# Products of bfloat16 zeros in the waits of a decoder layer

## The chip, the cores and the metric

The kernel runs on one core of one Trainium2 chip. The metric is the device time of one execution in microseconds (us); the figure of a version is the median of its runs. The kernel before took 1368.95 us (median of three runs: 1364.79, 1368.95 and 1383.22 us). The profile is of one further execution.

The engines are named as the profile names them: PE is the matrix engine (TensorE) and PEld its weight loads, DVE the vector engine, ACT the scalar engine, POOL the general one (GpSimd), SP the engine that here only starts transfers. PEclk is the clock that was granted to TensorE, as a share of its full speed.

## The reference

One decoder layer on x of 2 × 1024 tokens with 256 features, and a context of 2 × 77 tokens:

```
x = layernorm(x + causal_self_attention(x))       # 16 heads of 16, rotary positions, all float32
x = layernorm(x + cross_attention(x, ctx, mask))  # 16 heads, 77 keys, projections with biases
h = silu(x·w1·s1) * (x·w2·s2)                     # 256 -> 1024
h = gelu(h·h1·s)                                  # 1024 -> 1024
h = gelu(h·h2·s)                                  # 1024 -> 1024
x = layernorm(x + h·w3·s3)                        # 1024 -> 256
```

The weights of the feed forward are −1, 0 or 1 times a power of two, with a float32 scale for every output.

## The kernel before

**Tiling.** A tile is 128 tokens. The tokens are worked in five chunks (CHUNKS, line 31): tiles 0–1, 2–3 and 4–7 of the first sequence, then tiles 0–3 and 4–7 of the second. They are numbered 0 to 4 here.

**Stages of one chunk.** `project` (line 271, named `start(n)` where it is called) transposes x, forms q, k and v, turns q and k by their positions and transposes them by head. `maxima` (line 330, `top(n)`) forms causal scores tile by tile, takes each row's maximum on DVE (line 363) and puts it into a row of q through transposes of the padded tile `m_pad` (line 236), so that the next stage's scores come out with the maximum already subtracted. `values` (line 374, `weighted(n)`) goes through four groups of four heads, and in each through all tiles of keys: scores `su` (four heads in four row groups of the array, 17 rows each), exponential on ACT (line 410), weighting of the values into `po`. It runs one step behind itself: the weighting of step k − 1 is issued after the scores of step k. `self_finish` and `cross` (together `rest(n)`) finish the self-attention and do the cross-attention: projection, maxima (DVE `top`, line 470), exponential (line 491), weighting, projection, normalization. `feed_forward_exact` (line 632) is the feed forward on bfloat16 weights, with each float32 activation split in three bfloat16 planes; its products are recorded at line 91.

**Two parts.** The first part does the attention of chunk 0 and the projection of chunk 1. Beside it `survey` (line 695) reads the 22 slices of the feed forward's weights (512 KB each), finds out on DVE (line 704) whether bfloat16 holds them exactly, and writes a bfloat16 copy made by ACT to memory (line 706 and the transfer after it). Then a flag is read and one of two branches is taken. With these inputs it is the exact one; the other holds the same work in float32.

**What sets the order.** Every stage is a generator that yields an estimate in us after each step. In the branch, `beside` (line 736) draws steps of the attention as the work, and after each one lets the feed forward of earlier chunks run until the step's estimate is used up. `fed` (line 773) yields None while the chunk whose feed forward is next isn't through its cross-attention; then `beside` drops the credit and goes on, and the attention runs alone. In the first part `together` (line 724) interleaves streams by their pace. The kernel is then scheduled with the dependencies between tiles, and with order-only dependencies that `behind` adds (line 68): `tiled` keeps four products of one set together, and `filling` (line 90) keeps the feed forward from running further ahead than two steps of the attention. `latest[0]` is the last product that `matmul` (line 76, recorded at line 77) issued.

**Banks.** [...] `ps_u` takes four as one score tile, `ps_o` one, and `ps_f` three, which `bank()` (line 95) hands out in turn to everything else.

Of the kernel before, what the change touches and what calls it, by code (L numbers as in the profile page):

```python
# [10 lines left out]
BF16 = mybir.dt.bfloat16  # L11
# [8 lines left out]
P = 128  # L20
# [13 lines left out]
NEG = -3.0e38  # L34
EPS = 1e-5
AHEAD = 2


@with_exitstack
def kernel(ctx: ExitStack, tc: tile.TileContext, a: dict, out: bass.AP):  # L40
    nc = tc.nc
# [4 lines left out]
    const = pool("const")  # L46
# [7 lines left out]
    @contextmanager  # L54
    def part():

        with ExitStack() as mine:
            for name, bufs in (("small", 4), ("work", 2), ("probs", 2)):
                setattr(pl, name, mine.enter_context(tc.tile_pool(name=name, bufs=bufs)))
            for name, bufs in (("ps_u", 1), ("ps_o", 1), ("ps_f", 3)):  # L60
                setattr(pl, name, mine.enter_context(tc.tile_pool(name=name, bufs=bufs, space=PSUM)))
            yield mine
# [3 lines left out]
    marks, latest = [], [None]  # L66

    def behind(ins, other, reason):
        tc.add_manual_dep(
            ins,  # L70
            other.name,
            mybir.DependencyInfo(mybir.DependencyClass.NoSync, mybir.DependencyReason.DATA),
            reason=reason,
        )
# [15 lines left out]
    def filling(*args, **kw):  # L90
        ins = nc.tensor.matmul(*args, **kw).ins  # L91
        if len(marks) > AHEAD:
            behind(ins, marks[-1 - AHEAD], "no further ahead of the attention")

    def bank(name="pm"):
        return pl.ps_f.tile([P, 512], F32, tag="f", name=name)

    def scores_bank(name="su"):
        return pl.ps_u.tile([P, 4, 512], F32, tag="u", name=name)

    ident = const.tile([P, P], F32, name="ident")
    make_identity(nc, ident)
    ident_h = const.tile([P, P], BF16, name="ident_h")
# [54 lines left out]
    def heads_of(v):  # L158
        return v[..., : H * DV].rearrange("p (h d) -> p h d", h=H)

    def cross_keys():

        with ExitStack() as first:
            wkv = first.enter_context(tc.tile_pool(name="wkv", bufs=1))
            ctx_sb = wkv.tile([L, B, C], F32, name="ctx_sb")
            nc.sync.dma_start(ctx_sb, a["ctx"].rearrange("b l c -> l b c"))
            wk = wkv.tile([P, KC, NG, P], F32, name="wk")
            nc.sync.dma_start(wk, a["wkT"].rearrange("(k p) (g n) -> p k g n", p=P, g=NG))
            wv = wkv.tile([P, KC, C], F32, name="wv")
            nc.sync.dma_start(wv, a["wvT"].rearrange("(k p) n -> p k n", p=P))  # L170
            bv = wkv.tile([1, C], F32, name="bv")
            for w, name in ((bk, "bk"), (bv, "bv"), (bq, "bq"), (bo, "bo")):
                nc.sync.dma_start(w, a[name])
            mask_u8 = wkv.tile([P, NT, L], U8, name="mask_u8")
            nc.sync.dma_start(mask_u8, a["mask"].rearrange("(t p) l -> p t l", p=P))
            maskT_u8 = wkv.tile([L, T], U8, name="maskT_u8")
            nc.sync.dma_start(maskT_u8, a["maskT"])
            nc.sync.dma_start(wq, a["wqT"].rearrange("(k p) (g n) -> p k g n", p=P, g=NG))
            nc.sync.dma_start(wo, a["woT"].rearrange("(k p) n -> p k n", p=P))
            nc.vector.tensor_scalar(maskq, mask_u8, 1.0, -NEG, ALU.subtract, ALU.mult)  # L180
            nc.vector.tensor_scalar(maskk, maskT_u8, 1.0, -NEG, ALU.subtract, ALU.mult)
            nc.vector.tensor_scalar(bq, bq, 0.25, None, ALU.mult)
            for b in range(B):
                ct = wkv.tile([P, KC, L], F32, name=f"ctxT_{b}")
                pt = bank("pt")
                for k in range(KC):
                    nc.tensor.transpose(pt[:, k * L : (k + 1) * L], ctx_sb[:, b, k * P : (k + 1) * P], ident[:L, :L])
                nc.vector.tensor_copy(ct, pt[:, : KC * L].rearrange("p (k l) -> p k l", k=KC))
                yield 1
                pm = bank()  # L190
                for g in range(NG):
                    for k in range(KC):
                        matmul(
                            pm[:, g * P : g * P + L], wk[:, k, g, :], ct[:, k, :], start=(k == 0), stop=(k == KC - 1)
                        )
                for g in range(NG):
                    nc.scalar.activation(kx[b][:, g, :], pm[:, g * P : g * P + L], AF.Identity, bias=bk[:, g : g + 1])
                yield 1
                nc.gpsimd.memset(vx[b], 1.0)
                pm = bank()  # L200
                for k in range(KC):
                    matmul(pm[:L, :C], ct[:, k, :], wv[:, k, :], start=(k == 0), stop=False)
                matmul(pm[:L, :C], ones[:, :L], bv, start=False, stop=True)
                nc.scalar.copy(heads_of(vx[b])[:, :, :D], pm[:L, :C].rearrange("p (h d) -> p h d", h=H))
                yield 1
# [489 lines left out]
    def survey(flag):  # L695

        with ExitStack() as first:
            raw = first.enter_context(tc.tile_pool(name="raw", bufs=3))
            seen = raw.tile([P, N12 + 2 * NH + N3], F32, name="seen", bufs=1)
            for i in range(N12 + 2 * NH + N3):  # L700
                w = raw.tile([P, SLICE], F32, tag="w", name="w")
                nc.sync.dma_start(w, a["wf"][i])
                low = w.bitcast(U16).rearrange("p (n two) -> p n two", two=2)[..., 0]
                nc.vector.tensor_reduce(seen[:, i : i + 1], low, AX.X, ALU.max)
                h = raw.tile([P, SLICE], BF16, tag="h", name="h")
                nc.scalar.copy(h, w.bitcast(BF16).rearrange("p (n two) -> p n two", two=2)[..., 1])
                nc.sync.dma_start(wh[i], h)
                yield 1
            most = raw.tile([P, 1], F32, name="most", bufs=1)
            nc.vector.tensor_reduce(most, seen, AX.X, ALU.max)  # L710
            pm = bank()
            matmul(pm[:1, :1], most, all_ones, start=True, stop=True)
            nc.vector.tensor_scalar(flag, pm[:1, :1], 0.0, None, ALU.is_gt)
            yield 1
# [5 lines left out]
    def chain(*parts):  # L720
        for g in parts:
            yield from g

    def together(*streams):

        live = [[g, pace, 0.0] for g, pace in streams]
        while live:
            s = min(live, key=lambda s: s[2] / s[1])
            try:
                step = next(s[0])  # L730
                s[2] += step
                yield step
            except StopIteration:
                live.remove(s)

    def beside(work, filler):


        credit = 0.0
        for step in work:  # L740
            credit += step
            marks.append(latest[0])
            while credit > 0:
                credit -= next(filler, None) or credit
            yield step
        marks.clear()
        yield from filler

    def run(g):
        for _ in g:  # L750
            pass
# [6 lines left out]
    def start(n):  # L758
        yield from project(*CHUNKS[n], queries_of(n))

    def top(n):
        yield from maxima(*CHUNKS[n], queries_of(n))

    def weighted(n):
        osbs[n] = pl.work.tile([P, NG, CHUNKS[n][2] * P], F32, tag="osb", name="osb", bufs=1)
        yield from values(*CHUNKS[n], queries_of(n), osbs[n])
# [11 lines left out]
    def attention():  # L778
        for b in range(B):
            for t in range(NT):  # L780
                if b or t >= KT:
                    load_x(b, t)
        for i, name in enumerate(("w1_s", "w2_s", "h1_s", "h2_s")):
            nc.sync.dma_start(sc[:, i, :], a[name])
        nc.sync.dma_start(s3, a["w3_s"].partition_broadcast(P))

        nc.vector.tensor_scalar(sc[:, 0, :], sc[:, 0, :], 0.5, None, ALU.mult)
        nc.vector.tensor_tensor(sc[:, 1, :], sc[:, 0, :], sc[:, 1, :], ALU.mult)
        yield from together((rest(0), 1.0), (start(1), 0.2))
# [4 lines left out]
    flag = wcross.tile([1, 1], I32, name="flag")  # L794
    all_ones = const.tile([P, 1], F32, name="all_ones")
    nc.gpsimd.memset(all_ones, 1.0)
    with part():
        run(start(0))
        run(together((chain(top(0), weighted(0), cross_keys(), attention()), 1.0), (survey(flag), 0.8)))
    other_weights = nc.values_load(flag, min_val=0, max_val=1)  # L800

    def beside_each_other(forward, wbufs):
# [103 lines left out]
```

## Time and profile before

| what | value |
| --- | --- |
| median of the runs | 1368.95 us |
| the profiled execution | 1372.76 us |
| its span, first to last instruction | 1371.0 us |
| mean granted clock of TensorE over the span | 0.849 |
| PE busy | 1184.6 us, 86% of the span |
| DVE busy | 606.2 us, 44% |
| ACT busy | 378.9 us, 28% |
| POOL busy | 82.1 us, 6% |
| transfers | 54.89 MB in all |

The profiled execution is 3.8 us longer than the median. A share of busy time is a mean over stages that have different limits; the slices of the span and the chain of waits tell more. The chain is the work that ended last, followed back from the last instruction: at each step to what released it. In the lines of groups and of the timeline a product is given as out<-in with its tile names, and the tile shapes behind it; a bracket shows the idle time before it and what ended it. Times count from the start of the span.

### The profile page before, as it was taken

To read this page: it belongs to the slowest core of one execution; us is meant where nothing else is said; L and a number is where in the kernel's file an instruction comes from. 1 tells how busy PE (TensorE), PEld (TensorE's weight loads), DVE (VectorE), ACT (ScalarE), POOL (GpSimd) and SP (SyncE) were. 2 spreads that over 40 slices of the span, in tenths; PEclk is the share of its full clock that TensorE was granted. 3 is DMA by queue.
4 is the path that set the end of the run, shared out by engine and by line. 5 is a ranking of instruction groups with operands and counts; after the bars stand their busy time and mean duration, and the time that the engine had idled before them with its cause. 6 is when DMAs were issued, how large, how long until landed. Compare 5 with 4: busy or idle time off the path is not lost.

```text
span 1371.0 us, 17290 instructions
## 1 busy us (share of the span) xinstructions
PE 1184.6 (86%) x7542; PEld 577.2 (42%) x7602; DVE 606.2 (44%) x859; ACT 378.9 (28%) x413; POOL 82.1 (6%) x128
## 2 busy tenths in 40 slices
PE   5877899888987997887889997998789988899997
PEld 3443555654653212542433543435233244254444
DVE  6442823438764000531473454477931243338223
ACT  4331133231102444102035123111245630412221
POOL 1110001100000001100002100000001010000000
PEclk8576889987986558965589999999899998899999
DMA  9740111011211000000000000010100000012110
GB/s 312 246 146 0 32 40 39 25 39 32 70 47 39 1 0 0 1 1 1 0 16 16 23 16 24 16 31 32 31 16 24 24 16 16 16 32 62 47 50 22
DMA packets 30950, 54.89 MB, mean 40 GB/s; under 512 B 5033, under 2 KB 10258, under 8 KB 30866
## 3 DMA queue, kind: packets, MB, share of 16 engines
q1 hardware_dynamic: 30593, 52.91, 12.5%
q8 instruction: 61, 1.00, 0.3%
q10 hardware_dynamic: 272, 0.79, 0.2%
q14 instruction: 24, 0.19, 0.0%
HBM read 45.82 MB, written 7.86 MB: 39 GB/s over the span
## 4 chain that ended last, share of the span: by engine, by line
PE 67%; DVE 17%; ACT 10%; issue 3%; POOL 2%; DMA 1%; SPq 0%; ACTq 0%; POOLq 0%; DVEq 0%
PE pf L91 23%; PE su L77 19%; PE pm L77 7%; PE po L77 6%; DVE part L363 5%; ACT pr L410 4%; PE pq L77 2%; PE pu L91 2%; PE pg L91 2%; ACT pr L491 2%; DVE left L606 2%; DVE hid L609 1%; DMA w<-in_wf_dram 1%; PE pt L236 1%; PE pt L245 1%
## 5 line engine op out<-in xcount | busy, mean ns | idle before, releaser
L91 PEld LDWEIGHTS <-wf 128*128 128x128 bf16 x2400 | 229.2, 100 | 270.0 <-issue 111.5
L363 DVE TENSOR_REDUCE part<-su 128x4 f32<-128x2048 f32 (+3 forms) x76 | 165.3, 2175 | 55.0 <-PE su L77 54.7
L410 ACT ACTIVATE pr<-su 128x2048 f32<-128x2048 f32 (+1 forms) x104 | 140.5, 1351 | 171.7 <-PE su L77 171.0
L91 PE MATMUL pf<-mid,wf 128*128 128x512 bf16 (+1 forms) x625 | 167.4, 355 | 1.7 <-issue 1.2
L91 PE MATMUL pf<-hid,wf 128*128 128x512 bf16 (+1 forms) x620 | 161.8, 345 | 3.1 <-DVE gate L527 0.9
L77 PE MATMUL su<-q,kT 17*128 17x512 f32 (+3 forms) x832 | 116.5, 637 | 19.1 <-ACT pr L410 17.3
L77 PE MATMUL su<-kT,q 16*128 16x128 f32 (+3 forms) x1152 | 100.9, 470 | 32.4 <-DVE part L363 31.3
L77 PE MATMUL po<-pr,v 128*32 128x512 f32 (+3 forms) x832 | 106.3, 591 | 1.4 <-POOL pr L413 1.2
L91 PE MATMUL pf<-midm,wf 128*128 128x512 bf16 (+1 forms) x313 | 102.9, 346 | 0.8 <-issue 0.6
L91 PE MATMUL pf<-hidm,wf 128*128 128x512 bf16 (+1 forms) x313 | 101.3, 339 | 1.6 <-issue 1.4
L427 DVE COPY osb<-po 128x512 f32<-128x512 f32 (+1 forms) x20 | 11.7, 584 | 179.8 <-PE po L77 179.7
L77 PEld LDWEIGHTS su<-q,kT 17*128 17x128 f32 x832 | 40.4, 229 | 88.2 <-ACT pr L410 75.3
L77 PEld LDWEIGHTS su<-kT,q 16*128 16x128 f32 x1152 | 50.4, 225 | 64.2 <-DVE part L363 42.1
L413 POOL TENSOR_SCALAR_AFFINE_SELECT pr<-pr 128x512 f32<-128x512 f32 x64 | 40.7, 636 | 436.7 <-ACT pr L410 436.7
L606 DVE TENSOR_TENSOR left<-hid 128x1024 f32<-128x1024 f32 (+1 forms) x40 | 40.0, 1014 | 41.4 <-ACT hid L532 32.1
L534 DVE TENSOR_SCALAR mid<-pf,sc 128x256 f32<-128x256 f32 (+1 forms) x32 | 19.6, 615 | 82.7 <-PE pf L91 82.7
L491 ACT ACTIVATE pr<-su 77x2048 f32<-77x2048 f32 (+1 forms) x20 | 30.6, 1531 | 81.5 <-PE su L77 81.4
L91 PE MATMUL pg<-xTc,wf 128*128 128x512 bf16 (+1 forms) x157 | 50.7, 375 | 1.7 <-DVE xTc L228 0.9
L608 ACT COPY hidm<-left 128x1024 bf16<-128x1024 bf16 (+1 forms) x40 | 34.9, 875 | 58.1 <-DVE left L606 57.7
L91 PE MATMUL pu<-xTc,wf 128*128 128x512 bf16 (+1 forms) x156 | 50.3, 374 | 0.6 <-issue 0.5
L216 POOL TENSOR_SCALAR rstd<-mv 128x4 f32<-128x4 f32 (+1 forms) x15 | 4.4, 294 | 717.6 <-DVE mv L212 717.6
L470 DVE TENSOR_REDUCE top<-su 128x16 f32<-128x1232 f32 x16 | 23.1, 1442 | 54.2 <-PE su L77 54.2
(124 smaller groups left out, 1381.2 us busy)
## 6 DMA issues: line engine op xcount, KB each, us to landing
wf<-wh SPq DMA_DIRECT2D x110, 256.0 KB, 2.6
w<-in_wf_dram SPq DMA_DIRECT2D x22, 512.0 KB, 5.6
wh<-h SPq DMA_DIRECT2D x22, 256.0 KB, 2.8
x<-in_x_dram SPq DMA_DIRECT2D x16, 128.0 KB, 3.0
out_dram<-x SPq DMA_DIRECT2D x16, 128.0 KB, 1.8
wqkv<-in_w_qkv_dram ACTq DMA_DIRECT2D x1, 768.0 KB, 4.6
wk<-in_wkT_dram SPq DMA_DIRECT2D x1, 512.0 KB, 7.7
wq<-in_wqT_dram SPq DMA_DIRECT2D x1, 512.0 KB, 3.6
```

The costliest lines, as they stand in the source:

```text
L77: latest[0] = nc.tensor.matmul(*args, **kw).ins
L91: ins = nc.tensor.matmul(*args, **kw).ins
L236: nc.tensor.transpose(pt[:, g * P : (g + 1) * P], m_pad[:, 4 * g : 4 * g + 4, :].rearrange("p h d -> p (h d)"), ident)
L245: nc.tensor.transpose(pt[:, g * P : (g + 1) * P], osb[:, g, i * P : (i + 1) * P], ident)
L363: nc.vector.tensor_reduce(part[:, m, g0 : g0 + gm, :].rearrange("p g j -> p j g"), su[:, :, : gm * r].rearrange("p j (g r) -> p j g r", g=gm),
L410: nc.scalar.activation(pr[:, :, q0:], su[:, :, q0 : n * P], AF.Exp)
L413: nc.gpsimd.affine_select(out=pr[:, :, q0 : q0 + P], in_=pr[:, :, q0 : q0 + P], compare_op=ALU.is_ge, fill=0.0, base=0, pattern=[[0, 4], [ ...
L470: nc.vector.tensor_reduce(top.rearrange("p g j -> p j g"), su[:, :, : NG * L].rearrange("p j (g l) -> p j g l", g=NG), AX.X, ALU.max,)
L491: nc.scalar.activation(pr[:L], su[:L, :, : n * P], AF.Exp)
L534: nc.vector.tensor_scalar(nxt[:, f, :], pf, sc[:, s, f : f + 1], None, ALU.mult)
L606: nc.vector.tensor_tensor(left, x[:, k0:k1, :], upper[:, k0:k1, :], ALU.subtract)
L608: nc.scalar.copy(mid[:, k0:k1, :], left_upper)
```

## The change

A tile of zeros (128 × 512, bfloat16) is put into the constants, written once by DVE. A new function `keep_busy(us)` adds to an account of owed time and issues one product of zeros by zeros for every 0.215 us owed, into a bank drawn from `ps_f`; nothing reads that bank. The first product of a set is ordered behind the latest product of the attention. It is called at three places. In `beside`, where no feed forward is to be had, with 0.4 of the credit that is dropped. At the start of the first part, with 3 us. And after every step of the first part's attention, with 0.3 us and 0.4 of the step's estimate. The survey, the feed forward and all products that compute something are as before.

```diff
+BUSY = 0.4
+STEP_BUSY = 0.3
...
+    owed = [0.0]
+
+    def keep_busy(us):
+
+
+        owed[0] += us
+        n = int(owed[0] / 0.215)
+        if n <= 0:
+            return
+        owed[0] -= n * 0.215
+        to = bank("idle")
+        for i in range(n):
+            ins = nc.tensor.matmul(to, zeros[:, :P], zeros, start=True, stop=True).ins
+            if i == 0 and latest[0] is not None:
+                behind(ins, latest[0], "in the wait behind it")
...
+    zeros = const.tile([P, 512], BF16, name="zeros")
+    nc.vector.memset(zeros, 0.0)
...
             while credit > 0:
-                credit -= next(filler, None) or credit
+                took = next(filler, None)
+                if took is None:
+                    keep_busy(BUSY * credit)
+                credit -= took or credit
             yield step
...
+    def kept_busy(work):
+        for step in work:
+            keep_busy(STEP_BUSY + BUSY * step)
+            yield step
+
     with part():
-        run(start(0))
-        run(together((chain(top(0), weighted(0), cross_keys(), attention()), 1.0), (survey(flag), 0.8)))
+        keep_busy(3.0)
+        run(kept_busy(start(0)))
+        first = chain(top(0), weighted(0), cross_keys(), attention())
+        run(together((kept_busy(first), 1.0), (survey(flag), 0.8)))
```

## Prediction

> **What bounds the kernel now.** I read the page first: the slices of the span, then the chain by engine.
>
> ```profile
> PE   5877899888987997887889997998789988899997
> PEclk8576889987986558965589999999899998899999
> ...
> PE 67%; DVE 17%; ACT 10%; issue 3%; POOL 2%; DMA 1%; SPq 0%; ACTq 0%; POOLq 0%; DVEq 0%
> ```
>
> TensorE is the bound: busy in 86% of the span, 67% of the chain. One slice is 34.3 us. The granted clock is low in the first two slices and in two hollows: slices 13 to 16 (about 411 to 548 us) and 18 to 20 (583 to 685 us). From slice 21 on it is 0.95 over the stretch. Then I cut the span at the stages (columns: us, busy time and count of PE, weight loads, DVE, ACT, POOL, then granted clock, DMA share, GB/s):
>
> ```profile
> 45.00:76.00 31.00, 30.28 (x182) 16.38 (x183) 9.36 (x14) 15.01 (x25) 5.08 (x8) 0.50 0.69 223
> 76.00:146.00 70.00, 51.02 (x300) 29.53 (x293) 28.42 (x57) 14.35 (x23) 4.44 (x6) 0.72 0.17 56
> 436.70:545.00 108.30, 95.61 (x510) 21.95 (x511) 2.08 (x3) 50.19 (x33) 9.80 (x16) 0.59 0.00 1
> 545.00:590.00 45.00, 36.79 (x203) 21.21 (x201) 19.64 (x44) 8.80 (x19) 6.68 (x7) 0.97 0.00 1
> 590.00:697.00 107.00, 86.54 (x458) 41.90 (x460) 42.89 (x59) 10.21 (x10) 1.27 (x2) 0.51 0.00 1
> ```
>
> The third row is the values stage of chunk 2 (436.7 to 545). The fourth ends its self-attention and projects chunk 3. The last is cross-attention of chunk 2 beside the maxima of chunk 3. There is almost no feed forward in them. The chain of waits shows what a cold and a warm step cost:
>
> ```profile
> 477.73 2.13 PE su L77 x8
> ...
> 479.95 1.89 ACT pr L410
> 481.83 0.04 issue
> 481.88 2.13 PE su L77 x8
> ...
> 524.98 1.24 PE su L77 x8
> ...
> 526.30 1.89 ACT pr L410
> 528.18 0.04 issue
> 528.23 1.19 PE su L77 x8
> ```
>
> Scores, then their exponential, then the next scores, because there is one score tile. A cold step lasts 481.88 − 477.73 = 4.15 us; a warm one 528.23 − 524.98 = 3.25.
>
> **What raises the clock.** The bet is that products of zeros lift the clock. Rows of single clock windows (the record steps by 3.41 us) decide it:
>
> ```profile
> 475.70:479.10 3.40, 3.21 (x16) 0.62 (x16) 0.00 (x0) 1.88 (x1) 0.00 (x0) 0.50 0.00 0
> 516.60:520.00 3.40, 3.40 (x24) 0.72 (x16) 0.00 (x0) 1.82 (x2) 0.63 (x1) 0.50 0.00 0
> 523.50:526.80 3.30, 2.15 (x17) 0.61 (x17) 0.57 (x1) 1.93 (x2) 0.00 (x0) 1.00 0.02 5
> 827.30:830.60 3.30, 3.08 (x20) 1.79 (x14) 2.13 (x3) 0.00 (x0) 0.00 (x0) 0.50 0.00 0
> 830.70:834.00 3.30, 3.30 (x18) 1.59 (x16) 0.69 (x1) 0.00 (x0) 0.00 (x0) 1.00 0.00 0
> ```
>
> [...] 94% busy and still 0.50 afterwards. I therefore weight busy time by the rows that a product fills: scores fill 17 (or 16) rows in each of four row groups, 0.53; weighting with v, transposes and bfloat16 products fill 128 rows, 1. On this scale, which is my estimate, the cold windows that were followed by full clock lie at 0.82 or above (with exceptions either way up to 0.98), and warm ones fall below about 0.45. A cold step is (0.53 × 2.13 + 1.87) / 4.15 = 0.72: it stays cold. A warm one is (0.53 × 1.2 + 1.07) / 3.25 = 0.52: it stays warm, as row 523.50 does at 2.15 of 3.30 busy. So the stage sticks in the state it enters.
>
> Do zeros count? [...] But the window of 827.30 holds four transposes of m_pad (1.11 us), a tile of 31 zeros in 32 against an identity, and three bfloat16 products, and the clock rose after it. I take it that values don't matter. It is the weakest step: no product of zeros alone is in the trace.
>
> **The change part by part.** A product of 128x128 by 128x512 bfloat16 takes about 0.225 us warm and 0.43 to 0.48 cold (the feed forward's spacing in the chain; the causal mask's products). In the instruction order of the changed kernel there are 195 in the first part and 192 in the exact branch, which is the one that runs. Of the 192, some 12 are near 305 us and 180 between 425 and 690 us: elsewhere the feed forward fills the credit. All sums are against the profiled execution, 1372.76 us (span 1371.0), 3.8 above the median of 1368.95.
>
> *Values stage, 428 to 545.* The products come after the weighting of step k−1 and before the scores of step k+1, so in the wait for the exponential. A group of eight steps owes 0.4 × 9.4 / 0.215 = 17.5 products, 2.6 per full step. Cold, that step becomes 2.13 + 1.87 + 2.6 × 0.43 = 5.1 us, with 2.97 us of full rows in a row; a window that lies on it reaches (2.97 + 0.53 × 0.43) / 3.41 = 0.94 and lifts the clock, within three or four steps. Warm, 1.07 + 2.6 × 0.225 = 1.66 us lie under the 1.89 us exponential: hidden. A later stage has just this with five products:
>
> ```profile
> 1019.88 1.07 PE L77 MATMUL po<-pr,v 128*32 128x512 f32 x8
> 1020.11 1.88 ACT L410 ACTIVATE pr<-su 128x2048 f32<-128x2048 f32 x1 [1.42 <-PE su L77]
> ...
> 1022.10 1.14 PE L77 MATMUL su<-q,kT 17*128 17x512 f32 x8
> ```
>
> Groups of eight steps last 28.6 us cold and 22 warm. The 92 us from 428 to 520 are 3.2 groups: −21, less about 2.5 for the cold start: −18.5. Bounds −20 and −14; if the clock does not rise, 70 × 0.43 less the 4.5 us that cold waits hide, +25. What is late next is the exponential, 1.89 of 3.25.
>
> *545 to 590.* Already warm at 0.97, nothing to win. Some 25 to 30 products, most one at a time between short transposes and evacuations, each taking one of three PSUM banks, so that it waits for a bank and hands it on. 28 × 0.225 = 6.3, a little of it in waits: +5.5 (0 to +12).
>
> *590 to 697.* About 70 us of the chain are TensorE at 0.51; at the ratio 1.19 / 2.13 = 0.56 a warm stage would save up to 31. Some 80 products are added, in the waits for `top` (1.45 us), for `part` (2.3) and for the exponential (1.88). Against it: in the cross values a warm step is 77-row and 17-row work around a 1.88 us wait, at 0.43 on my scale with few products, so it falls cold again; then the products (cold four last 1.8 us, longer than the 1.45 of `top`) are on the path. I take maxima −5, cross values +1, rest −3: −7. Ends: −20 with the clock held, +15 with it never up.
>
> *Near 305 us*: 12 products in waits at the end of a cross-attention: 0.
>
> *First part, 0 to 146.* 13 products lead, on an engine that waits for x and weights: 0. Of the other 182 about 90 stand in waits. Three effects. The clock: rows 45.00 and 76.00 have 30.28 us at 0.50 and 51.02 at 0.72; with half of the cold work warm −4 to −12. The products on the path between 80 and 140 us: +8 to +13. And order: on TensorE the cross keys' products now follow the values instead of lying among them, on DVE a maximum stands behind the mask conversion (its DMA lands at about 42.7 us, +2.4), and on ACT the last exponential of the values and the copies of kx stand behind the conversions of weight slices 17 to 22, whose loads SP issues after the x loads, at 63 us. Some +4 to +7. I take +9 (+3 to +16). The memset of zeros: under 1 us of DVE while it waits for loads.
>
> *The rest, 697 to the end*: no product, clock 0.95: 0.
>
> Sum: −18.5 + 5.5 − 7 + 0 + 9 = −11, so 1361.8 on the profiled run's scale and 1358 on the median's.
>
> **The rivals.** (1) *Warm right through 590 to 697*, and a cheap first part: −18.5 + 5 − 20 + 2 = −31, about 1337. For: sticky states, and many full-row products in each wait there. Against: the 77-row steps. (2) *Slower: products of zeros don't count for the clock*, or not enough. Then every product is a cold 0.43 us and the engine that bounds pays it: values +25, 545 to 590 +6, 590 to 697 +15, first part +18: +64, about 1433. The point from which it decides is the share of a window that a zero product is worth: with nothing, a step has 3.0 of 5.1 us in weight, 0.59, and stays cold; it needs about half of full weight to pass 0.8. (3) *A wash*: clock gains and added products cancel, since banks and order cost in 545 to 697 and the first part what the values stage wins: about 1370.
>
> **How the numbers follow.** Forecast (1345 to 1365) 0.42; warm throughout 0.24; a wash, up to 1390, 0.2; slower 0.14. Two per cent, about what a measurement of this kernel tells from no change, is 27.4 us: 1341.6 and 1396.3. Two thirds of rival 1 and a tail of the forecast are faster by more: 0.22. Rival 2 and a tail of the wash, where the first part's queues cost over 20 us, are slower: 0.18. The range takes rival 1 and the wash, 1332 to 1392, and leaves rival 2 out.
>
> **What would show it.** Right: clock near 1.0 from about 440 to 545 us, steps of 3.25 us there, exponential ACT busy over half the stage; 545 to 590 longer by 5; 590 to 697 at a clock of 0.6 to 0.8, with falls in the cross values; the first part longer though its clock is higher. Wrong: 0.50 throughout the values stage with steps of 5.1 us (rival 2), or steps that stay at 4.15 (the products weren't in the wait), or 0.95 in 590 to 697 (rival 1).

## The result, and the profile after

The changed kernel took 1359.65 us (median of 20 runs, 1348.24 to 1367.11) against 1369.27 us for the kernel before (20 runs). The ratio is 0.9937, 95% interval 0.9912 to 0.9962: a gain of about 9 us, inside two per cent. The profiled execution took 1365.61 us, its span is 1363.9 us and its mean clock 0.918 (0.849 before). Its page, the slices of the span and the chain by engine:

```profile
PE   7798889988898888887889998998889989899997
PEclk8698996997998799987899999999899998899999
...
PE 63%; DVE 16%; ACT 11%; DMA 4%; issue 3%; POOL 2%; SPq 0%; ACTq 0%; DVEq 0%; POOLq 0%
```

Most of the hollow in slices 13 to 16 is gone, that in 18 to 20 is shallower. TensorE is still the bound, busy 88% of the span, of which 116 us are products of zeros. DMA, 1% of the chain before, is now 4%. By stages of the kernel after (us, busy time and count of PE, weight loads, DVE, ACT, POOL, then clock, DMA share, GB/s):

```profile
72.00:154.70 82.70, 71.13 (x463) 41.73 (x467) 29.82 (x59) 17.20 (x33) 4.44 (x6) 0.96 0.15 52
...
444.50:543.50 99.00, 84.40 (x607) 23.65 (x617) 7.57 (x13) 49.59 (x32) 10.50 (x17) 0.91 0.01 5
543.50:594.00 50.50, 45.54 (x250) 26.79 (x245) 19.95 (x44) 9.04 (x20) 6.98 (x7) 0.97 0.00 1
594.00:690.00 96.00, 77.47 (x525) 37.16 (x530) 42.78 (x60) 12.09 (x12) 1.28 (x2) 0.80 0.00 1
```

The first row answers to 76 to 146 us before (70 us at 0.72): the clock is nearly full and the stretch is longer all the same. The last row answers to the 107 us at 0.51 before. The second, the values stage of chunk 2 from the first work on it, answers to this stretch before, 18 us longer:

```profile
428.00:545.00 117.00, 100.63 (x550) 24.88 (x550) 7.56 (x13) 50.19 (x33) 10.73 (x18) 0.59 0.01 4
```

To say where time went I take the same DVE and ACT instruction in two profiles and note how much later it ends. Between six such marks, named by their place in the profile before, the differences are as follows (us; negative is a gain; each from one profiled execution against the same profile before):

| kernel | 0–148 | 148–430 | 430–548 | 548–592 | 592–722 | 722–1358 |
| --- | --- | --- | --- | --- | --- | --- |
| the change | +8.5 | +8.0 | −18.2 | +6.5 | −10.8 | −1.0 |
| branch only (e1) | +0.6 | −3.7 | −18.9 | +4.8 | −12.7 | −3.4 |
| first part only (e2) | +7.8 | −1.6 | +3.7 | +2.7 | −8.9 | −0.9 |
| quarter rows (e3) | +64.8 | −4.6 | +21.4 | +10.3 | +21.3 | −1.0 |
| branch only, weight values (e4) | +5.1 | +4.5 | −19.0 | +4.8 | −9.6 | +0.2 |
| first part only, one column (e5) | +7.8 | −3.4 | −2.1 | +2.8 | −7.2 | −0.3 |
| long steps (e6) | −0.5 | +4.7 | −18.9 | +2.8 | −9.9 | −6.2 |
| branch doubled (e7) | +2.5 | +4.8 | −19.5 | +9.5 | −6.1 | −4.8 |
| long steps and rest of chunk 0 (e9) | +10.2 | −4.0 | −18.9 | +4.0 | −8.0 | −0.7 |
| own bank (e10) | −5.2 | +9.1 | −18.5 | +4.6 | −9.4 | −3.6 |
| own bank, early (e12) | +0.3 | +4.6 | −18.4 | +4.3 | −12.6 | −3.6 |
| values stage only (e11) | +0.3 | −3.3 | −16.6 | +1.5 | −1.1 | −5.1 |

Three of the four runs of e2, its profiled one among them, lie over 1.5% above the fourth and count as slow, as do two runs of before (1383.22 here, 1385.6 beside e10 to e12).

The column from 148 to 430 is to be distrusted. There these kernels do nearly the same work in the same order, and they differ by up to 14 us. The values stage of chunk 1 lies in it, with 379 products on TensorE in either profile; it takes 47 us before (188 to 235) and 53.4 after (196 to 249.4). Its cold stretch lasted 13.7 us before:

```profile
188.90:202.60 13.70, 13.59 (x93) 5.52 (x93) 0.91 (x2) 4.52 (x6) 1.33 (x3) 0.50 0.05 11
```

After, 27.4 us:

```profile
198.90:226.30 27.40, 27.40 (x190) 11.60 (x182) 1.82 (x4) 7.34 (x8) 2.79 (x5) 0.50 0.08 20
```

TensorE is full in both. Weighted by rows filled, as the prediction does it (my estimate from the products in the two traces), the clock's windows in these stretches lie at 0.82 to 0.86, and only the last of each, after which the clock rose, at 0.90 and 0.94. So by this estimate the stage lies where the clock rises after some windows and not after others, and how the work falls in them may decide when. That this differs from run to run is what I infer from the runs of before (1360.69 to 1383.22 us); it isn't shown. The +8.0 of the change in that column is of this kind: e1, e2, e5 and e11 have −1.6 to −3.7 in its place, e4, e6, e7 and e12 have +4.5 to +4.8, and e10 +9.1. So a single difference between two profiles may be off by 4 to 9 us. In the first column, too, the five kernels whose first part has no products (e1, e4, e6, e7, e11) have −0.5 to +5.1. What follows leans on what several kernels repeat.

### The profile page after: what moved, and what is told of

Its sections match the earlier page's. It is cut to its first block, busy times and chain, and to the rows that moved or that the text cites. A ratio compares the mean times of both kernels' runs of the same rounds, so it can differ in the third digit from the quotient of the medians.

```text
span 1363.9 us, 18037 instructions
## 1 busy us (share of the span) xinstructions
PE 1197.6 (88%) x7895; PEld 586.0 (43%) x7989; DVE 608.2 (45%) x860; ACT 379.2 (28%) x413; POOL 82.3 (6%) x128
## 3 DMA queue, kind: packets, MB, share of 16 engines
q8 instruction: 64, 1.05, 0.3%
## 4 chain that ended last, share of the span: by engine, by line
PE 63%; DVE 16%; ACT 11%; DMA 4%; issue 3%; POOL 2%; SPq 0%; ACTq 0%; DVEq 0%; POOLq 0%
PE pf L93 24%; PE su L79 16%; PE pm L79 5%; DVE part L383 5%; ACT pr L430 5%; PE po L79 5%; DMA w<-in_wf_dram 3%; PE idle L109 3%; DVE left L626 2%; ACT pr L511 2%; PE pg L93 2%; PE pq L79 2%; PE pu L93 2%; DVE hid L629 1%; PE pt L256 1%
## 5 line engine op out<-in xcount | busy, mean ns | idle before, releaser
L109 PE MATMUL idle<-zeros 128*128 128x512 bf16 x353 | 116.1, 427 | 6.5 <-issue 3.1
L79 PE MATMUL su<-kT,q 16*128 16x128 f32 (+3 forms) x1152 | 90.4, 430 | 28.4 <-DVE part L383 28.1
L79 PE MATMUL su<-q,kT 17*128 17x512 f32 (+3 forms) x832 | 98.4, 545 | 18.9 <-ACT pr L430 16.7
L79 PE MATMUL po<-pr,v 128*32 128x512 f32 (+3 forms) x832 | 88.8, 502 | 2.2 <-POOL pr L433 1.6
L79 PEld LDWEIGHTS su<-kT,q 16*128 16x128 f32 x1152 | 44.5, 203 | 58.4 <-DVE part L383 38.5
L109 PEld LDWEIGHTS <-zeros 128*128 128x128 bf16 x387 | 36.3, 105 | 70.4 <-issue 55.5
L79 PEld LDWEIGHTS su<-q,kT 17*128 17x128 f32 x832 | 35.2, 198 | 63.6 <-ACT pr L430 50.6
```

Source lines behind the costliest of these rows:

```text
L79: latest[0] = nc.tensor.matmul(*args, **kw).ins
L109: ins = nc.tensor.matmul(to, zeros[:, :P], zeros, start=True, stop=True).ins
```

## Experiments

**The parts one by one.** e1 takes the first part's products out; e2 takes the branch's out.

```diff
 e1:
     with part():
-        keep_busy(3.0)
-        run(kept_busy(start(0)))
+        run(start(0))
...
-        run(together((kept_busy(first), 1.0), (survey(flag), 0.8)))
+        run(together((first, 1.0), (survey(flag), 0.8)))
 e2:
                 took = next(filler, None)
-                if took is None:
-                    keep_busy(BUSY * credit)
```

> The first part runs without products of zeros, the branch keeps its 192. My theory (three separate sums that add): the values stage of chunk 2 gains about 18 us, 545 to 590 loses 6, 590 to 697 gains 12, and the first part is as before: about 24 us below the time before, ratio 0.982 (0.978 to 0.987). Rival: the first part's products pay for themselves further on (a warm clock carried into the branch); then the ratio is that of the whole change, 0.994, or above.

> Only the 195 products of the first part, none in the branch; this leaves out the rest of the change. My theory: the first part ends 8 to 9 us later though its clock is higher, and the hollows of 428 to 520 and 590 to 697 us are back at 0.5: ratio 1.006 to 1.012. If the 8 us lost around 188 to 235 us follow from how the first part ends, they show here too; if they are chance of where the clock's windows fall, they need not. Rival (the first part gains by itself): ratio below 1.

e1: 1347.85 us, ratio 0.9865 (0.9807 to 0.9924), in the expected range. The branch is worth 0.0135 × 1371 = 18.5 us by the ratio and 23 by the medians, give or take 8 with four runs. The rival of e1, that the first part's warm clock pays further on, is out: its 0.994 lies above the interval.

e2: 1377.59 us (four runs from 1353.8 to 1386.71, so no ratio is given). The run of 1353.8 lies below every one of the 23 runs of before beside it (1359.32 to 1377.84), so the times of e2 alone don't show what the first part costs. Its profile loses 7.8 us there, the whole change's 8.5. Taken from e1's 18.5, 8 us leave about 10, near the whole's 9.6. The loss around 188 to 235 us is not in e2, although its first part ends as late as the change's: it doesn't follow from how the first part ends.

**Do zeros count, and what is counted?** e3 keeps number and length of the products and fills 32 rows in place of 128. e4 is e1 with the tile of zeros filled from w_qkv.

```diff
 e3:
-            ins = nc.tensor.matmul(to, zeros[:, :P], zeros, start=True, stop=True).ins
+            ins = nc.tensor.matmul(to, zeros[:32, :P], zeros[:32], start=True, stop=True).ins
 e4 (on e1):
-    nc.vector.memset(zeros, 0.0)
...
     nc.scalar.dma_start(wqkv, a["w_qkv"].rearrange("(k p) n -> p k n", p=P))
+    nc.vector.tensor_copy(zeros, wqkv[:, 0, :512])
```

> The changed kernel with products that fill 32 of the 128 rows, as many and as long as before. My theory, that busy time counts by the rows filled: a product is worth a quarter, a cold values step has (0.53 x 2.13 + 1.87 + 0.25 x 1.1) / 5.1 = 0.64 of full weight and stays cold; the step becomes about 5.1 us, 428 to 545 takes some 20 us more than before, and the whole is slower than before, ratio 1.02 to 1.05. Rival (what counts is that the array is busy, whatever its rows): the clock rises as with full rows, ratio 0.99 to 1.0.

> The kernel of the branch's products alone, with the tile of zeros filled with w_qkv rounded to bfloat16, so that the unread products multiply real numbers. My theory (the values don't matter): clock and stages as with zeros, 428 to 545 again 18 us shorter, ratio 0.982 to 0.990. Rival (switching counts for the clock): the hollows that remain with zeros, 17 us at the start of the values stage and about 45 us in 590 to 697, shrink, and the ratio falls to 0.975 or below; or real data draw a lower clock, and it rises.

e3: 1486.91 us, ratio 1.0877 (1.0793 to 1.0961). Two stages of it, the end of the first part and the values stage:

```profile
73.00:211.00 138.00, 130.61 (x470) 56.13 (x470) 29.30 (x59) 16.23 (x32) 4.43 (x6) 0.54 0.09 31
490.00:630.00 140.00, 137.50 (x635) 42.24 (x635) 6.70 (x9) 50.11 (x33) 10.98 (x18) 0.50 0.01 2
```

TensorE is busy in 137.50 of 140 us and the clock stays at 0.50 throughout. With 128 rows of zeros, the same stage in the change is busy in 84.40 of 99 us at 0.91. So in this stage busy time alone didn't raise the clock, 128 rows filled did where 32 didn't, and rows of zeros counted. The values stage lost 21.4 us as expected (some 20); the whole lost 1.0877 in place of the expected 1.02 to 1.05, because the first part lost 64.8 us.

e4: 1347.65 us, ratio 0.9832 (0.9768 to 0.9896); the values stage gains 19.0 us, as with zeros (18.9). In this stage real numbers did no more and no less than zeros. The whole can't be told from e1: the intervals overlap.

**The first part: order or time?** e5 keeps the first part's products, banks and all, but makes each one column wide; the branch has none.

```diff
-    owed = [0.0]
+    owed, WIDTH = [0.0], [1]
...
-            ins = nc.tensor.matmul(to, zeros[:, :P], zeros, start=True, stop=True).ins
+            ins = nc.tensor.matmul(to[:, : WIDTH[0]], zeros[:, :P], zeros[:, :WIDTH[0]], start=True, stop=True).ins
```

> The first part's products alone, each of one column in place of 512, so that their banks and their places in the order stay and their time nearly goes; none in the branch. It parts the first part's 8.7 us into order and time. If the order costs them (cross keys after the values, a maximum behind the mask's load, copies behind the conversions of weight slices): still 4 to 8 us later at the end of the first part, at a low clock, ratio 1.003 to 1.008. If the products' own time costs them, the first part ends as before or within 2 us: ratio 0.998 to 1.002.

e5: 1379.06 us (20 runs), ratio 1.006 (1.0034 to 1.0086), as expected if order costs. Its profile loses 7.8 us by the end of the first part, as many as e2's, with 15.7 us of products in the first part in place of the change's 58.9. But it doesn't lose them in the same place. How much later than before three marks of DVE come (us; the last copy of the values, at 76.9 before; `rec`, the first step behind the values and the cross keys, at 78.2; the end of the first part, at 147.9):

| kernel | last copy | `rec` | end |
| --- | --- | --- | --- |
| the change | −3.4 | +7.9 | +8.5 |
| e2 | −3.2 | +8.3 | +7.8 |
| e5 | −9.3 | +1.2 | +7.8 |
| e9 | +1.2 | +1.2 | +10.2 |
| e10 | −4.7 | −4.2 | −5.2 |
| e12 | −3.7 | −3.7 | +0.3 |
| no products there (e1, e4, e6, e7, e11) | −1.9 to +1.6 | −1.9 to +1.6 | −0.5 to +5.1 |

The change loses 11.3 us between the values and `rec`, and next to nothing after it. e5 loses 6.6 of its 7.8 after it, at a lower clock. The stretch from `rec` to the end, before, in e5 and with the change:

```profile
78.20:148.00 69.80, 52.27 (x301) 30.73 (x302) 28.59 (x55) 13.39 (x22) 4.44 (x6) 0.71 0.15 48
79.40:155.80 76.40, 61.06 (x394) 38.06 (x393) 27.73 (x54) 11.84 (x21) 4.44 (x6) 0.63 0.07 25
86.10:156.40 70.30, 59.84 (x392) 34.69 (x398) 25.51 (x51) 11.11 (x20) 4.44 (x6) 0.94 0.06 19
```

So that e5 and the change both end some 8 us late is a coincidence, and e5 doesn't show that order alone makes up the change's loss. It does show that the order moves. In its chain:

```profile
67.97 2.01 PE pm L79 x16
...
70.03 1.51 PE pm L79 x6
...
72.62 2.21 PE pm L79 x16
...
74.91 2.89 PE pm L79 x6
```

The last copy of the values is done at 67.57 us (76.91 before), and then the cross keys' products, 8.6 us, stand alone on the path; before, they lay between the steps of the values. In e5 the values gain about what the keys then cost. In the change itself a wait is added. Its chain:

```profile
73.42 5.34 DMA w<-in_wf_dram
...
78.79 1.22 DVE seen L724
80.01 0.23 DVE ctxT L208
...
80.29 2.01 PE pm L79 x16
```

On DVE the copy of the second context's transposes (ctxT) comes after the survey of a weight slice (seen) that is still on its way, and the keys wait for the copy. It ends at 80.24 us, 6.7 after the last copy of the values; in the timeline of the kernel before, the same copy is at 57 us:

```profile
57.06 0.32 DVE L188 COPY ctxT<-pt 128x154 f32<-128x154 f32 x1 [1.06 <-PE pt L187]
```

**Another bank.** The order moved although `keep_busy` adds only one dependency to a set. What else it takes is a bank of the three that the keys' transposes need too, while the values draw none of them; with products behind the values, a bank for the keys can come free only after products that are ordered behind the values. This is a reading of the code. e10 draws the first part's products from `ps_o`, which stands idle outside the values stages, and puts none behind the values and the cross keys; e12 does it only up to the maxima of chunk 0.

```diff
 e10 (on e1; e12 leaves attention() as it was):
-        to = bank("idle")
+        to = pl.ps_o.tile([P, 512], F32, tag="o", name="idle") if pool == "o" else bank("idle")
...
-        run(start(0))
-        first = chain(top(0), weighted(0), cross_keys(), attention())
+        keep_busy(3.0, "o")
+        run(kept_busy(start(0)))
+        first = chain(kept_busy(top(0)), weighted(0), cross_keys(), kept_busy(attention()))
```

> All of the branch's products, and in the first part products behind the steps of projection, maxima, finishing and cross-attention (none behind the values and cross keys), drawn from the bank of ps_o instead of the three that everything else shares. In the instruction order the cross keys then stay among the values and DVE's and ACT's work stays almost as before. My theory (the first part lost by the shared banks, which move the keys and the copies behind the weight slices, not by the products themselves): the first part ends 0 to 5 us earlier than before in place of 8.5 later; ratio 0.975 to 0.985. Rival (the products' own time on the path): still 5 us or more later, ratio 0.988 to 0.995.

> The same with products only in the projection and maxima of chunk 0, none from the values on, so it parts the start (waits for loads) from the finishing of chunk 0. My theory: the clock is up until the values begin, 3 to 6 us earlier there, and half of it is left at the end of the first part, since the cross keys wait for their loads; ratio 0.978 to 0.986. Rival (order): 2 us or more later than before.

e10: 1345.88 us, ratio 0.9853 (0.9825 to 0.9882), at the edge of what my theory said. e12: 1347.07 us, ratio 0.9869 (0.9842 to 0.9897), a little above it. In the timeline of e10 the copy is back in its place:

```profile
55.75 0.31 DVE L208 COPY ctxT<-pt 128x154 f32<-128x154 f32 x1
```

and the first part ends 5.2 us earlier than before, against 8.5 later with the change. e12 ends it 0.3 us later than before, which neither its theory nor its rival said: it is 3.7 early at `rec` and loses that after it. e10 is the fastest in median of all kernels here, and its interval and e12's lie wholly below that of the change, so what the change does in the first part costs time; against e1 and e12 e10 can't be told apart. Of the 13.7 us between it and the change 12.1 are there at `rec`, so they belong to what happens up to the keys. e10 changes two things at once, the bank and where the products stand. No run has the change's places with another bank, so which of the two keeps the keys in place stays open.

**Products on the path.** e9 puts products, from the shared banks, only behind the cross keys of the first part; in the branch both e6 and e9 have them only behind steps of over 0.6 us.

```diff
 e6 (on e1):
-                if took is None:
+                if took is None and step > 0.6:
 e9 (on e6):
-        first = chain(top(0), weighted(0), cross_keys(), attention())
+        first = chain(top(0), weighted(0), cross_keys(), kept_busy(attention()))
```

> The branch's products alone, and only behind steps of more than 0.6 us of attention, so that the short steps of projection and finishing get none. My theory (behind the short steps a product stands on the path, 5 us of it in 545 to 590): that stage is as before, the values stage and the cross maxima keep their gain, 5 us below the kernel with all of the branch's products, ratio 0.977 to 0.985. Rival (those products hold the clock up into 590 to 697): the cross stage falls cold and the gain of 13 us there goes, ratio 0.988 or above.

> Products behind the long steps of the branch, and in the first part only from the end of the cross keys on (rest of chunk 0 and projection of chunk 1), so that what stands before them keeps its order. If the first part loses by its order alone, this stretch now gains from the clock: 76 to 146 us is 3 to 6 us shorter than before. If the products' time on the path there eats the clock's gain: within 3 us of before, or longer. I expect the latter, and a ratio equal to that of the long steps alone, 0.977 to 0.987.

e6: 1348.14 us, ratio 0.9848 (0.9787 to 0.9909): in the expected range, but not to be told from e1, where I expected 5 us less; with four runs of each, 5 us can't be ruled out. In the profiles the short steps' products cost some 2 us (+4.8 in e1 against +2.8 in 548 to 592). Kernels with no products at all there (e2, e5, e11) have +1.5 to +2.8 too: about 2 us of the loss seem to lie in the one profile of before.

e9: 1356.15 us, ratio 0.9914 (0.9879 to 0.995), 8 us slower than e6 in the median and 10.5 in the profile, though the intervals overlap; I expected no difference in the whole. Its keys are in their place (the copy at 58 us), so this loss isn't the late keys. The stretch from the end of the keys to the end of the first part, in e9:

```profile
89.80:158.00 68.20, 60.31 (x365) 33.11 (x365) 22.22 (x41) 10.00 (x18) 3.16 (x5) 0.83 0.07 21
```

and in e10:

```profile
83.60:142.70 59.10, 53.49 (x356) 30.63 (x363) 22.27 (x41) 9.66 (x18) 3.16 (x5) 0.94 0.08 25
```

Both have over 70 products there, and they are 30% and 29% of the chain: some 21 and 17 us stand on the path, not in waits. At 0.94 the clock pays for them (0.8 us shorter than before), at 0.83 it doesn't (8.4 longer). By these means some 23 us of e9's stretch and 7 of e10's were at 0.50: e9 has cold windows at 110, 124 and 131 to 141 us, e10 only at its first and last. Whether the shared bank or chance sets e9's cold windows isn't known.

**How many fit in a wait?** e7 doubles the branch's products.

```diff
 on e1:
-BUSY = 0.4
+BUSY = 0.8
```

> The branch's products alone, twice as many (0.8 of the dropped credit in place of 0.4). In a full values step 5.2 products of 0.225 us and 1.07 us of weighting are 2.24 us, over the 1.89 us of the exponential: each full step becomes about 0.4 us longer, 8 us in the stage; 545 to 590 loses another 6; 590 to 697 is warmer (up to 10 less) but has 80 products more (up to 18 more). My theory (the products' time is free only while it fits in a wait): worse than with 0.4, ratio 0.99 to 1.0. Rival (more activity is worth more): below 0.985.

e7: 1358.63 us, ratio 0.9923 (0.9887 to 0.9959), within the expected range and for half of the expected reason. Its chain in the values stage:

```profile
472.08 1.07 PE su L79 x8
473.15 0.99 PE po L79 x8
474.14 1.19 PE idle L109 x5
475.33 1.07 PE su L79 x8
```

The exponential is gone from the chain: scores, weighting and five products now fill the step, 475.33 − 472.08 = 3.25 us. That is what the step took before with its wait. The wait is used up exactly, the hollow at the stage's start is gone (the clock is 1.00 from 437 to 536 us), and the stage gains 19.5 us, as with half of the products. That stage was to get 8 us longer by my theory, and didn't. The extra products cost in 548 to 592 (+9.5 against e1's +4.8) and in 592 to 722 (−6.1 against −12.7).

**What the cross stage brings.** e11 allows products in the values stages only, by a switch set around `values`.

```diff
 on e1:
-                if took is None:
+                if took is None and in_values[0]:
...
+        in_values[0] = True
         yield from values(*CHUNKS[n], queries_of(n), osbs[n])
+        in_values[0] = False
```

> Products in the branch only while a values stage runs; none in finishing, projection, maxima and cross-attention, none in the first part. In the two kernels without products in the branch, the stretch of 592 to 691 us was 7 to 8 us shorter than in the profile of before too, so what the cross stage's products bring is open. If they bring the 8 to 13 us read from the profiles: this kernel loses them, ratio 0.990 to 0.994 and 0.5 through most of 590 to 690. If that was chance of the clock's windows: the values stage's 19 us are the whole gain, ratio 0.983 to 0.989, equal to the branch's products within 3 us.

e11: 1349.5 us, ratio 0.9883 (0.9853 to 0.9914), on the same chip and beside the same runs of before as e10 and e12. Its cross stage:

```profile
574.20:681.00 106.80, 88.12 (x464) 42.51 (x465) 43.42 (x61) 11.41 (x11) 1.27 (x2) 0.52 0.00 1
```

106.8 us at 0.52: as before. With products, in e1:

```profile
575.00:673.40 98.40, 82.14 (x543) 38.61 (x543) 46.95 (x65) 13.04 (x13) 1.28 (x2) 0.81 0.01 3
```

e11's median is 2.4 to 3.6 us above e12's and e10's. The table has −8 to −13 with about 0.4 of the credit in products, but −7.2 and −8.9 in e5 and e2 without any, where e11, without any there as well, has −1.1; what shortened it in those two isn't shown. So the products there are worth a few us, less than a single pair of profiles says; how many stays open. The values stage alone carries most of the gain.

## Why the prediction was right, and where not

*The values stage*: −18.5 predicted, −18.2 measured. The step is as forecast. The chain after:

```profile
484.08 1.19 PE su L79 x8
...
485.35 1.89 ACT pr L430
...
487.28 1.19 PE su L79 x8
```

487.28 − 484.08 = 3.20 us, 3.25 forecast. The stage begins cold and is warm from 461.8 us, two cold steps in; three or four were forecast. The weakest step held: zeros count (the stage at 0.91 with them, 0.59 before), and with e4's 19.0 us for real weights against 18.9 for zeros, a clock that zeros can't raise is out for this stage.

*What raises the clock*: the scale by rows filled was an estimate from the trace before. There the window at 475.70 us, busy in 3.21 of 3.40 us, was followed by one just as busy (479.10 to 482.50) and again at 0.50. e3, 98% busy at 0.50 in the values stage, shows again that being busy wasn't enough there, and against the change's 0.91 that the rows mattered. The scale holds over all thirteen traces. Of their cold windows (3.41 us each, at a clock of 0.50), weighted by my estimate from the products in them, none of 514 below 0.70 was followed by full clock, 97 of 167 between 0.82 and 0.90 were, and 242 of 253 at 0.90 or more. Of 257 that TensorE filled to over 98% but that reach less than 0.80 in weight, 4 were. So no sharp threshold shows on this scale, and the values stage of chunk 1, at 0.82 to 0.86, lies where the clock rose after some windows and not after others.

*545 to 590*: +5.5 predicted, +6.5 measured; but about 2 of it belong to the profile before, and only 2 to 4 to the products, by the kernels with and without them. Their number on the path was put too high. In the trace after, the 34 products of this stage waited once, 1.2 us, and not for a bank; the bank waits I named there weren't the cost.

*590 to 697*: −7 predicted, −10.8 measured up to 722, of which the runs leave a few us to the products. The size was right only with the luck of one profile.

*The first part*: +9 predicted, +8.5 measured, in other shares. I had the clock at −4 to −12, the products on the path at +8 to +13 and the order at +4 to +7. In the profile the change is 3.4 us early when the values are done and loses 11.3 by `rec`, while the keys stand behind the values, as forecast, and wait for a slice. After `rec` the products are on the path as forecast, but the clock (0.94 against 0.71) pays for them: +0.6. So products and clock cancel there, and the order seems to cost more than I put: e10, with the keys in place, is 12.1 us earlier at `rec`. How much of this is order and how much the products behind the values the runs don't part. Of the order, the piece that I named as copies of kx and an exponential behind slices 17 to 22 was, in the chain, the copy of ctxT on DVE behind the survey of a slice.

*148 to 430*: 0 predicted, +8.0 in the profile. Other kernels with the same work there have −4.6 to +9.1. So I put it down to chance.

*Rival 2* (slower, 1433) is what e3 is: no rise of the clock. The values stage lost 21.4 where +25 was said. The mis-sized term is the first part: +18 said, +64.8 measured. The prediction's own figures give more than 18: the 92 products that it left outside waits, at a cold 0.43 us, are 40 us. In e3 the products take 52.5 us of TensorE between 73 and 211 us alone, at 0.54; that few waits are left to hide them when everything is cold is my reading.

*The sum*: −11 predicted, −9.6 measured between the medians and −7.1 between the profiles. That the sum of the profiles is so near is in part luck: +8.0 of chance before 430 us stands against 3.8 more than forecast in the cross stage and 1.0 after it.

## What to carry to other kernels

Here work that nobody reads paid in a stage that a wait left at the low clock: in the values stage the clock went from 0.59 to 0.91, for 18.2 us. It was free up to the length of that wait at the high clock (five products, 1.19 us of a step of 3.25 us in e7), and the rows it filled counted: with 128 the clock rose, with 32 it stayed at 0.50. Look at what such work takes besides time: products in the first part moved copies and keys that the change never names (the copy of ctxT from 57 to 80 us), perhaps by the banks that they share, which no run shows alone. And before a stage's gain is credited to a change, look at the same stage in kernels that don't touch it, and at where in the stage two kernels gain or lose: two equal sums can have different causes.

## What the runs showed of the hardware

- Products of zeros over 128 rows raised the clock in the values stage from 0.59 to 0.91; zeros over 32 rows, with TensorE busy 137.50 of 140 us, left it at 0.50; rows of real weights gained 19.0 us there, zeros 18.9.
- Over the thirteen traces the rows filled in a cold window told better than its busy time whether full clock followed: by the estimate above it did after 242 of 253 windows at 0.90 or more, but after only 4 of 257 that were busy to over 98% and weighed less than 0.80.
- The same stage, with 379 products either time, stayed cold with TensorE full for 13.7 us (188.9 to 202.6, before) or for 27.4 us (198.9 to 226.3, after). I had not expected that profiles of nearly the same work differ by up to 14 us between 148 and 430 us.
